# Two step boundaries between a norm and its transposes, and an order for the transposes, in the last attention of a sequence kernel

## The chip, the cores and the metric

The kernel runs on one core of a Trainium2 chip. A core has five engines that work side by side, each through its own instructions in order: TensorE (PE in the profile, with its weight loads shown apart as PEld), VectorE (DVE), ScalarE (ACT), GpSimd (POOL), and SyncE (SP), which here only issues DMAs. The metric is the device time of one execution in microseconds (us); lower is better.

## The reference, cut to what matters

The reference is a chain of eight residual layers on 8 sequences of 256 tokens with 128 channels, each followed by a layer norm without gain. The change touches the end of it: the mixture of experts that is the sixth layer (its norm), the attention that is the seventh, and the ternary linear layer that is the eighth. In the reference's words:

```
x = _layernorm(x + _L2_ffn_ref(x, ...))           # experts: shared + two routed per token
x = _layernorm(x + _L3_attn_ref(x, w_qkv, w_o, log_xi))
x = _layernorm(x + _L3_ffn_ref(x, weight, alpha, bias))
...
scores = einsum('bhqd,bhkd->bhqk', q, k) * dh ** (-0.5) + bias   # 16 heads of 8, causal, some heads with decay
attn = softmax(scores);  out = einsum('bhqk,bhkd->bhqd', attn, v);  return out @ w_o
```

So for every sequence there are three norms over channels in this last part: after the experts, after the attention, and after the linear layer.

## The kernel before, in words

The kernel runs six stages one after another. The change lies in the last two, `moe2` (the experts) and `typed` (the attention, with the linear layer behind it). A norm works with tokens on partitions, so that a token's mean and variance lie along one partition; the matmuls that follow need channels on partitions. Each norm is therefore followed by two 128x128 transposes on TensorE.

**The norm.** `token_norm` (L468) takes statistics for two blocks of 128 tokens on VectorE (L474, L475), a logarithm and an exponential on ScalarE for the reciprocal root (L477, L478), then gives control back once (`yield`), and then scales and shifts both blocks on VectorE (L481: two instructions in the profile's "L481 ... x2"). `channels` (L483) takes one PSUM bank (tag M, of which this stage has one), transposes the two blocks into it on TensorE (L487, tile `zt`) and copies the bank to SBUF (L488, on VectorE or ScalarE as its caller says).

**The turns of `typed`.** Each of the 8 sequences gives six units of attention: two for the first 128 queries (four pairs of heads each, 8 groups of 128 keys) and four for the second 128 queries (4 groups of 256 keys). The loop takes one turn `i` per unit and is software-pipelined. Turn `i` gives out, in this order:

1. the transposes of the weights of unit `i-3` (L507, tile `pt`, with copies `ptsb` at L509 on whichever of VectorE and ScalarE the scheduler picks);
2. the scores of unit `i` on TensorE (tile `sc`, two PSUM banks A in all);
3. the softmax of unit `i-1`: maximum on VectorE (L1766, `nm`), exponentials on ScalarE (L1771), reciprocal of the sums on VectorE (L1773, `rc`; this one is also remembered as `self.paced`), and the multiply by it on GpSimd (L1774, tile `e`);
4. two steps of side work;
5. the outputs of unit `i-3` on TensorE (tile `o`, 16 matmuls);
6. one more step of side work.

The side work comes from a queue of generators; a step runs the front one to its next `yield`. There are three kinds:

- `results(b)` finishes the experts of sequence b: four VectorE instructions that add two gathered, weighted rows to the shared part (L1638, "combine" below), the first norm, its transposes and the copy `x_moe`. The first instruction of each pair is held behind `self.paced`, the reciprocal given out last.
- `before(b)` makes that sequence's attention inputs: two projections (`proj`), the products for q and k, the masked keys `km` on GpSimd (L1726), and v.
- `after(b)`: the output projection (`wo`), residual and second norm (L1824, L474 to L481), its transposes and the copy `s_t`, a bias add on GpSimd (L1829), the linear layer (`lin`), residual (L1836), third norm, its transposes and the copy out.

I count turns within a sequence as turn 3 to turn 8: in turn 3 the outputs of a sequence's first unit come, in turn 8 those of its sixth. `results(b+2)` enters the queue in turn 3, `before(b+2)` and `after(b)` at the end of turn 8. The first sequence's `results` and first `before` run during the last parts of `moe2`, between the chunks of the shared expert (`shared`, L1550 and on: `pg`, `pu`, L1571 `sh`, `acc`), the second's at the start of `typed`.

**What sets the order.** The program order is a priority, not the final order. A compile-time scheduler walks a modelled time and gives each engine, whenever it is free, the ready instruction of highest priority; copies written as `nc.any` rank lower and go to either engine. The result is a fixed queue per engine, and on the chip an instruction that has to wait holds up all behind it on its engine. `issue_after(later, earlier)` adds an edge without a semaphore: it only forbids the scheduler to place `later` before `earlier`.

Of the kernel before, what the change touches and what calls it, by code (L numbers as in the profile page):

```python
# [21 lines left out]
P = 128  # L22
# [284 lines left out]
class _Kernel:  # L307
    def __init__(self, ctx, tc, ins, out):
# [67 lines left out]
        self.places = [self.dram.tile([2560, P], F32, name=f"places{i}") for i in range(2)]  # L376
        self.scatters = [], []


    def v(self, name, j=0, n=1):  # L380
        c = _V[name] + j
# [101 lines left out]
    def channels(self, z, dst, copy, tag="M"):  # L483

        ps = self.psum(tag, "zt")
        for t in range(2):
            self.nc.tensor.transpose(ps[:, t * P : (t + 1) * P], z[:, t, :], self.ident)  # L487
        copy(dst, ps[:, 0:S])  # L488

    def softmax(self, small, work, sc, groups, keys, tag):  # L490
# [1048 lines left out]
    def moe2(self):  # L1539
        nc, tc = self.nc, self.tc  # L1540
        E, CAP = 8, 320
        x = self.x
        y = self.xs.tile([P, T], F32, tag="x", name="x_moe2")
        ws = self.ws
        gu, down = self.wsh

        keep = self.pool("keep")
        self.typed_start()
        with (
            tc.tile_pool(reuse_waits="tile", name="m2", bufs=1) as one,  # L1550
            tc.tile_pool(reuse_waits="tile", name="m2w", bufs=2) as work,
        ):
            ss = []

            def shared(i):
                cs = bass.ts(i, 512)
                acc = self.psum("S", "acc")
                s = keep.tile([P, 4, P], F32, name=f"s{i}")
                nc.sync.dma_start(s, self.zrows[512 * i : 512 * (i + 1), :].rearrange("(t p) d -> p t d", p=P))
                ss.append(s)  # L1560
                for c in range(8):
                    pg, pu = self.psum("A", "pg"), self.psum("A", "pu")
                    self.mm(pg, gu[:, 0, c * P : (c + 1) * P], x[:, cs])
                    self.mm(pu, gu[:, 1, c * P : (c + 1) * P], x[:, cs])
                    h = work.tile([P, 512], F32, tag="sh", name="sh")
                    self.silu = nc.scalar.activation(h, pg, AF.Silu)
                    if self.norm:

                        self.issue_after([self.silu], self.norm)
                        self.norm = None  # L1570
                    self.paced = nc.vector.tensor_mul(h, h, pu)  # L1571
                    for t in range(4):
                        ts = slice(t * P, (t + 1) * P)
                        self.mm(acc[:, ts], h[:, ts], down[:, c * P : (c + 1) * P], c == 0 and t == 0, c == 7 and t == 3)
                    yield
                s = s.rearrange("p t d -> p (t d)")
                nc.vector.tensor_add(s, acc, s)


            self.norm = None  # L1580
            common = shared(0)
            for _ in range(2):
                next(common)
            for _ in self.rest:
                pass
            bt, group = self.rows_of(one, 1)
            for _ in common:
                pass
            ybuf = self.dram.tile([E * CAP, P], F32, name="ybuf2")
            groups = 0  # L1590
            for e in range(E):
                w = ws.pop(0) if ws else self.weights2(e)
                while 512 * groups < CAP * (e + 1):
                    group(groups)
                    groups += 1
                xe = bt[:, e * CAP : (e + 1) * CAP]
                h = work.tile([P, 4, CAP], F32, tag="h", name="h")
                for c in range(4):
                    pg, pu = self.psum("A", "pg"), self.psum("A", "pu")
                    self.mm(pg[:, :CAP], w[:, 0, c * P : (c + 1) * P], xe)  # L1600
                    self.mm(pu[:, :CAP], w[:, 1, c * P : (c + 1) * P], xe)
                    nc.scalar.activation(h[:, c, :], pg[:, :CAP], AF.Silu)
                    nc.vector.tensor_mul(h[:, c, :], h[:, c, :], pu[:, :CAP])
                ys = work.tile([P, 3, P], F32, tag="ys", name="ys")
                py = self.psum(name="py")
                for i, n in enumerate((P, P, CAP - 2 * P)):
                    for c in range(4):
                        self.mm(py[0:n, i * P : (i + 1) * P], h[:, c, i * P : i * P + n], w[:, 2, c * P : (c + 1) * P], c == 0, c == 3)
                nc.any.tensor_copy(ys[:, 0:2, :].rearrange("p a b -> p (a b)"), py[:, 0 : 2 * P])
                nc.any.tensor_copy(ys[0:64, 2, :], py[0:64, 2 * P : 3 * P])  # L1610
                r0 = e * CAP
                nc.sync.dma_start(ybuf[r0 : r0 + 2 * P, :].rearrange("(a p) d -> p a d", p=P), ys[:, 0:2, :])
                nc.sync.dma_start(ybuf[r0 + 2 * P : r0 + CAP, :], ys[0:64, 2, :])
            got = [[], []]

            def fetches():


                for t in range(NT):
                    for k in range(2):  # L1620
                        got[k].append(self.gather(keep, ybuf, self.get2[:, k], t, f"got{k}{t}"))
                        if t > 1:
                            self.wait_for(self.gathered, self.silu)
                            yield

            fetch = fetches()
            next(fetch)

            def results(b, work):

                z = self.rows(b)
                if b == 0:
                    self.exp_ln(self.silu)
                for j in range(2):
                    t = 2 * b + j
                    for k in range(2):

                        i = nc.vector.scalar_tensor_tensor(z[:, j, :], got[k][t], self.gate2[:, k, t : t + 1], z[:, j, :], ALU.mult, ALU.add)  # L1638
                        if k == 0:
                            self.issue_after([i], self.paced)  # L1640
                yield from self.token_norm(z, z, self.tys)
                yield
                self.channels(z, y[:, bass.ts(b, S)], nc.vector.tensor_copy)

            self.results = results
            self.rows = lambda b: ss[b // 2][:, b % 2 * 2 : b % 2 * 2 + 2, :]
            for _ in shared(1):
                next(fetch)
            self.x = y
            first = chain(results(0, self.ty), self.typed_before(0))  # L1650
            for i in (2, 3):
                for _ in shared(i):
                    next(first, None)
                    next(fetch, None)
            for _ in chain(first, fetch):
                pass
            self.exp_ln(self.silu)
# [83 lines left out]
    def typed_scores(self, unit, q, km, decay, last):  # L1741

        t, r0, r1 = unit
        keys, nr = P * (t + 1), r1 - r0
        sc = self.psum("A", "sc", 1024).rearrange("p (j r k) -> p j r k", j=2, r=nr)
        half = [slice(64 * j, 64 * j + 64) for j in range(2)]
        line = [self.mm(sc[:, j], q[h, t * P : (t + 1) * P], km[h, r0:r1, 0:keys], True, False) for j, h in enumerate(half)]
        for j, h in enumerate(half):  # L1750
            line.append(self.mm(sc[:, j, 1::2, :], self.onesb[h, :], decay[h, r0 // 2 : r1 // 2, 0:keys], False, False))
        for j in range(2):
            line.append(self.mm(sc[:, j, :, keys - P : keys], self.identb, self.m("causal").unsqueeze(1).to_broadcast([P, nr, P]), False, True))
        for i in line:
            if last is not None:
                self.issue_after([i], last)
            last = i
        return sc, last

    def typed_softmax(self, unit, sc, work, small):  # L1760
# [20 lines left out]
    def typed_outputs(self, unit, pts, vm, o, last):  # L1781
        t, r0, r1 = unit
        for i in range(4):
            r, kt = r0 + i // (t + 1), i % (t + 1)
            for j, pt in enumerate(pts):
# [6 lines left out]
                )  # L1792
                if last is not None:
                    self.issue_after([m], last)

    def typed_start(self):
        one, self.ty, self.tys = self.pool("ty1"), self.pool("ty", 2), self.pool("tys", 6)
# [11 lines left out]
    def typed(self):  # L1809
# [3 lines left out]
        def after(b, o):  # L1813
# [4 lines left out]
            ps = self.psum("M", "wo")[:, 0:S]  # L1818
            for t in range(2):
                ts = slice(t * P, (t + 1) * P)  # L1820
# [3 lines left out]
            nc.vector.tensor_add(flat(s), ps, flat(self.rows(b)))  # L1824
            yield from self.token_norm(s, s, small)
            yield
            st = work.tile([P, S], F32, tag="st", name="s_t")
            self.channels(s, st, nc.scalar.copy)
            nc.gpsimd.tensor_tensor(s, s, self.bias3.unsqueeze(1).to_broadcast([P, 2, P]), ALU.add)  # L1829
            yield  # L1830
            ps = self.psum("M", "lin")[:, 0:S]
            for t in range(2):
                ts = slice(t * P, (t + 1) * P)
                self.mm(ps[:, ts], st[:, ts], we, t == 0, t == 1)
            s2 = work.tile([P, 2, P], F32, tag="s2", name="s2")
            nc.vector.tensor_add(flat(s2), ps, flat(s))  # L1836
            yield from self.token_norm(s2, s2, small)
            yield
            s3 = work.tile([P, S], F32, tag="s3", name="s3")
            self.channels(s2, s3, nc.scalar.copy)  # L1840
# [75 lines left out]
```

## Time and profile before

| quantity | value |
|---|---|
| median of 3 runs | 1842.15 us (1837.2 to 1847.08) |
| the profiled execution's own time | 1842.98 us |
| span of the profiled execution | 1840.4 us |
| mean granted TensorE clock | 0.925 |
| PE busy over the span | 1529.9 us (83%) |
| DVE, ACT, POOL busy | 1111.1, 1002.1, 587.6 us |
| PE busy, 1680 to 1720 us | 36.84 of 40 us, granted clock 1.00 |
| PE busy, 1800 to 1841 us | 25.43 of 41 us, granted clock 0.86 |

The stage `typed` runs from about 1590 us to the end, at 29.1 us per sequence in the middle. A row of a timeline gives the start in us, the duration in us, the engine, the source line, the operation, output<-inputs, shapes and the count of merged instructions; in square brackets stands how long the engine was idle before, and what released it. A line such as L404 is a helper's, so one goes by the tile's name.

### The profile page before, as it was taken

Reading aid. Unit: us, or ns where it says so; the run is one execution under the profiler, and the core shown is the slowest. Engines: PE = TensorE matmul, PEld = TensorE weight load, DVE = VectorE, ACT = ScalarE, POOL = GpSimd, SP = SyncE. Lnnn points to the kernel's source line nnn. Section 1 sums busy time; section 2 is a strip of 40 time slices with the busy share of each in tenths; the row PEclk is TensorE's granted clock in tenths of the full one; section 3 lists DMA queues with packets and bytes.
Section 4 is the critical chain, followed back from the end, with each engine's and each line's share of the span. In section 5 each row is a group of like instructions: output and inputs, shape, how many; then the busy total and the mean of one; then the engine's idle time right before and its main releaser. Section 6 shows DMA issues by size and latency. Waiting matters only on the chain.

```text
span 1840.4 us, 28746 instructions
## 1 busy us (share of the span) xinstructions
PE 1529.9 (83%) x10858; PEld 941.3 (51%) x10858; DVE 1111.1 (60%) x2158; ACT 1002.1 (54%) x2690; POOL 587.6 (32%) x535
## 2 busy tenths in 40 slices
PE   3667887878788878778479999999996998899996
PEld 2244544544444444344266666666654665456564
DVE  5724458778787776967624556554545222577775
ACT  4556777667767795666134444444444222355553
POOL 1314434343434324110412122211213004456562
PEclk7798998989999989888779999999998999999998
DMA  4000002020202031246530000000101320000000
GB/s 178 1 1 1 1 23 59 13 70 24 70 24 70 24 92 36 58 153 207 133 105 7 4 13 10 9 4 8 40 4 36 79 67 26 18 4 4 7 7 6
DMA packets 63049, 77.97 MB, mean 42 GB/s; under 512 B 6108, under 2 KB 39924, under 8 KB 61888
## 3 DMA queue, kind: packets, MB, share of 16 engines
q1 hardware_dynamic: 57584, 70.03, 13.2%
q0 software_dynamic: 3216, 5.07, 1.0%
q8 instruction: 85, 1.39, 0.3%
q10 hardware_dynamic: 2112, 1.05, 0.2%
q14 instruction: 52, 0.43, 0.1%
HBM read 66.87 MB, written 10.76 MB: 42 GB/s over the span
## 4 chain that ended last, share of the span: by engine, by line
PE 50%; DVE 19%; ACT 12%; issue 8%; POOL 8%; DMA 2%; another core or an unknown queue 0%; SPq 0%; DVEq 0%; POOLq 0%; ACTq 0%
PE vps L404 7%; PE sc L404 6%; PE kps L404 5%; PE pt L507 4%; PE out L404 3%; DVE hs L832 3%; PE o L404 3%; PE pu L404 3%; ACT e L679 3%; PE pg L404 3%; DVE hs L833 2%; PE y L404 2%; DVE hs L830 2%; PE py L404 2%; PE hps L404 2%
## 5 line engine op out<-in xcount | busy, mean ns | idle before, releaser
L404 PE MATMUL y<-hs,ident 128*128 128x512 f32 x256 | 147.9, 707 | 40.3 <-DVE hs L833 40.0
L832 DVE TENSOR_TENSOR_SCAN hs<-da,hs 128x1024 f32<-128x1024 f32 x64 | 153.5, 2405 | 1.8 <-ACT da L828 1.6
L507 PE MATMUL pt<-ident,e 128*128 128x128 f32 x768 | 120.6, 287 | 28.0 <-POOL e L684 13.8
L684 POOL TENSOR_TENSOR e<-e,rc 128x1024 f32<-128x1024 f32 x32 | 67.7, 2116 | 234.0 <-DVE rc L683 233.8
L828 ACT ACTIVATE da<-d,na 128x255 f32<-128x255 f32 x256 | 111.8, 501 | 40.0 <-DVE hs L832 21.6
L1771 ACT ACTIVATE e<-sc,nm 128x128 f32<-128x128 f32 (+1 forms) x256 | 103.7, 432 | 44.8 <-DVE nm L1766 44.8
L679 ACT ACTIVATE e<-sc,nm,rn 128x128 f32<-128x128 f32 x256 | 113.4, 463 | 26.6 <-DVE nm L674 24.1
L507 PEld LDWEIGHTS pt<-ident,e 128*128 128x128 f32 x768 | 87.9, 144 | 66.0 <-issue 19.9
L631 POOL TENSOR_TENSOR t<-t,t 128x512 f32<-128x512 f32 x64 | 91.0, 1421 | 93.9 <-DVE t L618 78.3
L1774 POOL TENSOR_TENSOR e<-e,rc 128x1024 f32<-128x1024 f32 x48 | 92.0, 1918 | 90.0 <-DVE rc L1773 77.5
L830 DVE TENSOR_TENSOR hs<-u,bc 128x1024 f32<-128x1024 f32 x64 | 86.3, 1358 | 34.8 <-POOL u L817 29.4
L1322 ACT COPY kp<-kps 128x512 f32<-128x512 f32 x128 | 74.5, 585 | 54.5 <-PE kps L404 53.3
L1171 POOL DMA_INDIRECT got<-ybuf,get x48 | 45.8, 955 | 179.6 <-DMA ybuf<-ys 88.3
L404 PEld LDWEIGHTS y<-hs,ident 128*128 128x128 f32 x256 | 51.8, 217 | 98.5 <-DVE hs L833 54.9
L509 ACT COPY ptsb<-pt 128x512 f32<-128x512 f32 x91 | 53.2, 586 | 82.4 <-PE pt L507 73.2
L1347 POOL TENSOR_TENSOR e<-e,rc 128x512 f32<-128x512 f32 x32 | 33.5, 1048 | 198.7 <-DVE rc L1346 90.9
L509 DVE COPY ptsb<-pt 128x512 f32<-128x512 f32 x101 | 67.4, 678 | 33.5 <-PE pt L507 33.4
L404 PE MATMUL qk<-w_local,h 128*128 128x512 f32 x128 | 70.4, 638 | 14.1 <-DVE t L618 9.9
L833 DVE TENSOR_TENSOR hs<-hs,bc 128x1024 f32<-128x1024 f32 x64 | 80.2, 1259 | 0.2
L636 PE MATMUL qkt<-ident,t 128*128 128x128 f32 x256 | 44.0, 292 | 28.2 <-POOL t L633 20.4
L1571 DVE TENSOR_TENSOR sh<-sh,pu 128x512 f32<-128x512 f32 x32 | 22.0, 688 | 75.1 <-PE pu L404 56.6
L1358 ACT COPY vs<-vps 128x512 f32<-128x512 f32 x64 | 37.3, 583 | 54.4 <-PE vps L404 49.2
(384 smaller groups left out, 3868.4 us busy)
## 6 DMA issues: line engine op xcount, KB each, us to landing
bc<-xs SPq DMA_DIRECT2D x128, 256.0 KB
w_attn<-in_w_dram SPq DMA_DIRECT2D x4, 1024.0 KB
w_local<-in_w_dram SPq DMA_DIRECT2D x2, 1557.0 KB
places<-zeros SPq DMA_DIRECT2D x2, 1280.0 KB
w_moe<-in_e1gate_dram SPq DMA_DIRECT2D x8, 256.0 KB
w_moe<-in_e1up_dram SPq DMA_DIRECT2D x8, 256.0 KB
w_moe<-in_e1down_dram SPq DMA_DIRECT2D x8, 256.0 KB
w_moe<-in_e2rg_dram SPq DMA_DIRECT2D x8, 256.0 KB
```

The costliest lines, as they stand in the source:

```text
L404: return self.nc.tensor.matmul(out, lhsT, rhs, start=start, stop=stop)
L507: self.last = self.nc.tensor.transpose(pt[:, j * P : (j + 1) * P], src[:, j * P : (j + 1) * P], self.ident)
L509: self.nc.any.tensor_copy(sb.rearrange("p a b -> p (a b)"), pt)
L631: nc.gpsimd.tensor_add(t1, t1, t2)
L679: nc.scalar.activation(e[:, j, g, :], scs[:, j, g, :], AF.Exp, bias=nm[:, j, g : g + 1], scale=rq[:, j, g : g + 1], accum_out=sm[:, j, g : ...
L828: nc.scalar.activation(da[:, n, c, 1:S], d[:, c, 1:S], AF.Exp, scale=na[:, i : i + 1])
L830: nc.vector.tensor_tensor(hs, u.unsqueeze(1).to_broadcast(shp), bn, ALU.mult)
L832: nc.vector.tensor_tensor_scan(line(hs), line(da), line(hs), 0.0, ALU.mult, ALU.add)
L833: nc.vector.tensor_tensor(hs, hs, cn, ALU.mult)
L1322: self.copied = nc.scalar.copy(k[:, 2 * i : 2 * i + 2, :].rearrange("p a b -> p (a b)"), ps)
L1771: nc.scalar.activation(e[:, i, :], sc[:, i, :], AF.Exp, bias=nm[:, i : i + 1], accum_out=sm[:, i : i + 1])
L1774: nc.gpsimd.tensor_tensor(e, e, rc.unsqueeze(2).to_broadcast([P, n, keys]), ALU.mult)
```

## The change

It does two things. First, in the three places where a norm's scalings are followed by its transposes (`results`, and twice in `after`), a second `yield` stands between them, so that two boundaries between steps lie there and not one. Second, `channels` holds each transpose behind `self.fed`, the TensorE instruction that was given out last by the scores, the outputs or the shared expert's last matmuls, with an edge of order alone. `self.fed` is `None` until `shared` first runs, so an earlier caller of `channels` is untouched.

```diff
@@ __init__
         self.scatters = [], []
+        self.fed = None
@@ channels
         ps = self.psum(tag, "zt")
         for t in range(2):
-            self.nc.tensor.transpose(ps[:, t * P : (t + 1) * P], z[:, t, :], self.ident)
+            i = self.nc.tensor.transpose(ps[:, t * P : (t + 1) * P], z[:, t, :], self.ident)
+            if self.fed:
+                self.issue_after([i], self.fed)
         copy(dst, ps[:, 0:S])
@@ shared, in moe2
                         ts = slice(t * P, (t + 1) * P)
-                        self.mm(acc[:, ts], h[:, ts], down[:, c * P : (c + 1) * P], c == 0 and t == 0, c == 7 and t == 3)
+                        self.fed = self.mm(acc[:, ts], h[:, ts], down[:, c * P : (c + 1) * P], c == 0 and t == 0, c == 7 and t == 3)
@@ results, in moe2
                 yield from self.token_norm(z, z, self.tys)
                 yield
+                yield
                 self.channels(z, y[:, bass.ts(b, S)], nc.vector.tensor_copy)
@@ typed_scores
             last = i
+        self.fed = last
         return sc, last
@@ typed_outputs
                     self.issue_after([m], last)
+        self.fed = m
@@ after, in typed
             yield from self.token_norm(s, s, small)
             yield
+            yield
             st = work.tile([P, S], F32, tag="st", name="s_t")
...
             yield from self.token_norm(s2, s2, small)
             yield
+            yield
             s3 = work.tile([P, S], F32, tag="s3", name="s3")
```

## The prediction

> **What bounds the kernel now.** I read the page's engine row, then the busy time by stretches of the last attention, then what TensorE waited for there, then the timeline of one sequence.
>
> ```profile
> PE 1529.9 (83%) x10858; PEld 941.3 (51%) x10858; DVE 1111.1 (60%) x2158; ACT 1002.1 (54%) x2690; POOL 587.6 (32%) x535
> ```
>
> ```profile
> 1680.00:1720.00 40.00, 36.84 (x298) 23.84 (x300) 30.32 (x68) 25.71 (x120) 23.09 (x15) 1.00 0.01 4
> 1800.00:1841.00 41.00, 25.43 (x206) 16.89 (x202) 19.92 (x46) 13.82 (x53) 10.92 (x7) 0.86 0.02 7
> ```
>
> The columns of the stretches are width, then busy time of PE, PEld, DVE, ACT and POOL, then granted clock, DMA share and GB/s. In the steady part TensorE is busy 36.84 of 40 us; no other engine passes 31. So TensorE's idle gaps are all that there is to win there. The waits of TensorE, 1611 to 1800 us, have one row for our transposes (total, times, longest):
>
> ```profile
> PE zt L487 <- DVE s L481: 11.2, 18, 1.4
> ```
>
> The timeline shows where they fall. One sequence of 29.1 us, TensorE first, in turns 6 to 8:
>
> ```profile
> 1646.45 0.49 PE L487 MATMUL zt<-ident,s 128*128 128x128 f32 x2 [0.42 <-DVE s L481]
> 1646.87 1.09 PE L404 MATMUL o<-ptsb,vm 128*64 128x128 f32 x16
> ...
> 1650.09 0.61 PE L404 MATMUL sc<-msk,identb 128*128 128x512 bf16 x2
> 1652.10 0.59 PE L487 MATMUL zt<-ident,s 128*128 128x128 f32 x2 [1.40 <-DVE s L481]
> 1652.61 1.09 PE L404 MATMUL o<-ptsb,vm 128*64 128x128 f32 x16
> ```
>
> The first wait is the third norm's (of `after`), the second the first norm's (of `results`). The VectorE and GpSimd rows say why the second is long:
>
> ```profile
> 1645.96 0.60 DVE L481 TENSOR_SCALAR s<-s,mv,rs 128x128 f32<-128x128 f32 x2
> 1646.47 0.17 DVE L1773 RECIPROCAL rc<-sm 128x4 f32<-128x4 f32 x1
> 1646.56 2.75 DVE L1638 SCALAR_TENSOR_TENSOR s<-got,gate,s 128x128 f32<-128x128 f32 x4
> ...
> 1650.90 0.66 DVE L509 COPY ptsb<-pt 128x512 f32<-128x512 f32 x1
> 1651.70 0.60 DVE L481 TENSOR_SCALAR s<-s,mv,rs 128x128 f32<-128x128 f32 x2
> ```
>
> ```profile
> 1646.79 2.11 POOL L1774 TENSOR_TENSOR e<-e,rc 128x1024 f32<-128x1024 f32 x1 [3.06 <-DVE rc L1773]
> ```
>
> The combine takes 2.75 us here while GpSimd multiplies; at 1588.16, with no such multiply running, the same four took 1.13. It loses 1.62 us, and it does so because it stands right behind a reciprocal, which releases a multiply 0.3 us later. The scalings L481 show the same: 0.60 alone, 1.86 at 1610.51 and 1.82 at 1804.23, where a reciprocal had just gone.
>
> The gaps, listed: 1.40 five times (1652 to 1768), 0.42 six times (1646 to 1792), 0.15 six times (second norm), 0.83 once at 1612.18: 7.0 + 2.5 + 0.9 + 0.8 = 11.2, the row above. Outside it: 1.70 and 1.90 at 1805.94 and 1812.94 for the last sequence but one; 2.20 and 2.27 for the last, which has nothing left to put in between; 0.50 and 0.52 around the transposes at 1544.24 in the experts' stage. All that can move adds to 7.0 + 2.5 + 0.9 + 0.8 + 3.6 + 1.0 = 15.8 us, 0.86% of the time.
>
> **The change part by part.** No arithmetic instruction is added or removed; the edges are order on one engine and need no semaphore, cost 0.
>
> *Does the side queue hold?* A generator takes its yields plus one step. `results` goes from 3 to 4, `after` (its first step is taken at once) from 7 to 9, `before` stays 5: 15 become 18, and a sequence has 6 turns of 3 steps, 18. It just fits, so nothing piles up; but the queue no longer runs empty, and this moves the start of `results` too. Before, the combine was given out at the end of turn 6, behind the reciprocal of turn 6; now `after` is not done until turn 7, so the combine comes in turn 7, behind turn 7's reciprocal. Its transposes come in turn 8, not 7. The boundary bought is partly spent at the start of the chain. The other moves: the linear layer goes from the middle of turn 5 to its end, behind the outputs; the third norm's scaling from the end of turn 5 to turn 6, its transposes to the end of turn 6, behind the outputs; the store (SP's queue) to turn 7, where the transposes' result is ready and nothing waits for it. GpSimd's queue keeps its order except at the start. `before` stays in its place, at the end of turn 8.
>
> *Third norm, six times.* Its scaling ends at 1646.5 while the 16 outputs (1.02) now run first. The outputs need their copies `ptsb`, the last of which ends at 1646.03, so they run 1646.1 to 1647.1, and the transposes find their input there: 0.35 of 0.42 gained, -2.1. Ends: -2.5; or, if the reciprocal goes ahead of the scaling, it grows by 1.26 (1.86 less 0.60), reaches 1647.9, and the gap is 0.8: +2.3.
>
> *The linear layer behind the outputs.* Its result is awaited by the residual add L1836, which waits longer for the bias add on GpSimd (1643.00 + 0.73). `lin` would end at about 1643.3: cost 0. Were that add earlier, up to 0.8 (the ten outputs moved ahead) would fall on the third norm, and the 1.02 of outputs ahead of its transposes would take it up.
>
> *First norm, five times.* Scores in turn 6 end at 1645.95. Turn 7's maximum, no longer behind the combine, takes 1646.6 to 1647.8, its 8 exponentials about 3.0 (0.34 to 0.41 apiece): the reciprocal goes at about 1651.0 and the combine right behind it, with the multiply on its heels: 2.75, to 1653.9. Statistics and ScalarE's two take 1.2, the scaling 0.60: transposes at 1655.75 at the earliest. TensorE, 0.35 early, has turn 8's scores done at 1653.95 and the outputs at 1654.97. So at least 0.8 us of gap is left: -0.6 each, -3.0. From above: the two `ptsb` copies of turn 8 (1.3) and a maximum (1.2) want VectorE in the same stretch behind the blocked combine; with the copies alone the scaling ends at 1657.1 and the gap is 3.2, +1.8 each, +9.0. Between these ends I take 1.6, the part of the combine that only the multiply explains: the schedule is made without it, I infer, for its order would otherwise not leave TensorE idle there; whatever place it picks, this lag lands on TensorE. That is +0.2 each, +1.0.
>
> The Trainium skill, "SBUF — State Buffer", section "Who interferes with whom", speaks against the change here: VectorE (with two SBUF inputs) and GpSimd share a port pair as an exclusive lock, and the loser blocks for the whole instruction. The combine would then cost 1.13 + 1.89 = 3.02 where the row says 2.75, and this sum would be 0.27 x 5 = 1.4 us worse; the row decides.
>
> *Second norm, six times:* same order (scores, transposes, outputs): 0.
>
> *Last sequence but one.* The first gap, 1.70, gets the other 14 outputs (about 0.95) ahead of it: -0.95. The second transposes come a whole turn later: -1.90. Together -2.85; some comes back, as TensorE then waits for the last softmaxes (0.35, 0.23 and 0.29 from 1819 on): I take -2.0, ends 0 and -3.6.
>
> *Start.* At 1612.18 ten more outputs (0.80) go ahead: -0.8, ends 0 and -0.83. The second sequence's first transposes move behind the scores of the next unit and push `km` (3.75 on GpSimd) later; TensorE waits 2.80 at 1606.61 for a multiply behind it. Either that multiply slips ahead (-2.8) or another falls behind (+1.9, one multiply). Between the two: 0.
>
> *Experts' stage.* One chunk later the scaling is long done: -0.5; ends 0 and -1.0, both gaps.
>
> Sum: -2.1 + 1.0 - 2.0 - 0.8 - 0.5 = -4.4 us. The profiled execution took 1842.98 (its span is 1840.4), which gives 1838.6; that execution is 0.83 above the median of the runs, which gives 1837.8. I say 1838.
>
> **The rivals.**
>
> *The gaps close (gain over 0.5%).* For it: two boundaries give 1.02 to 4.7 us more work ahead of the transposes. Against: the combine's later reciprocal. With the lower ends, -2.1 - 3.0 - 2.85 - 0.8 - 1.0 - 2.8 = -12.6: 1830; if the 7.0 vanish whole, -16.6: 1826. It holds from the point where the first norm's scaling ends before 1655.0 on the old scale.
>
> *The gap widens in turn 8 (slower).* The copies `ptsb` queue behind the blocked combine, TensorE stands 3.2 us: +9.0. After the 2.80 gap at 1606.61 the next scores took 2.60 from start to outputs (1607.63 to 1610.23) against 1.50 at 1614.51, and the stretch 1600 to 1640 has a granted clock of 0.96 against 1.00: +1.1 each, +5.5. With the other terms (-5.4): +9.1, 1852 by the profile's time, 1851 by the median. For it: VectorE's full stretch; against: gaps of 1.70 and 1.90 slowed nothing. It is slower than before when the gap passes 1.40 by 1.1 (5.4 over five).
>
> The Trainium skill, "TensorE: Matmul & The Clock Gate", section "Why this matters for your kernels", puts the drop of the clock at idle gaps above about 3 us; here 2.80 already slowed it. By the page the 5.5 stays for a gap of 3.2 and falls away for one of 2.8.
>
> *The order comes out as before,* if the scheduler's times leave the transposes where they were: 1842.
>
> **How the numbers follow.** Chances: forecast 0.40, gaps close 0.28, gap widens 0.22, no change 0.10. The forecast's own range is 1834 to 1842: the term of the first norm between -3.0 and +5.0 (a gap of 2.4), the rest as summed. The whole range is 1828 to 1854: below to the middle of the first rival, above to the second with the start's +1.9. Half a per cent, 9.2 us, is about what a measurement of this kernel can tell from no change. Faster than that: the first rival and a little of the forecast, 0.30; slower: most of the second, 0.22; within: 0.48.
>
> **What would show it.** Right: the transposes of the third norm stand behind 16 outputs with no gap; the combine stands behind a reciprocal of 128x8, not 128x4, at 2.75 again; the gap of 1.40 turns up in turn 8, before `zt` or `o`, at about 1.6. Wrong: a period clearly under 28.6 or over 30 us; `ptsb` copies on ScalarE all through turn 8; a granted clock under 1.00 in the steady part; scalings of 1.8 in it.

## The result, and the profile after

The changed kernel takes **1871.11 us** (median of 4 runs, 1868.33 to 1873.65), the kernel before, run beside it, 1844.62 us (1837.2 to 1847.74): a ratio of **1.0143**, 95% interval 1.0123 to 1.0162. It is slower by some 26.5 us. The forecast was 1838 and the range ended at 1854, so the prediction was wrong in sign and in size. The second rival named the place of the loss, but priced it at 1851.

The profiled execution of the changed kernel took 1872.6 us, its span is 1870.7. Engine row of its page:

```profile
PE 1546.2 (83%) x10858; PEld 956.9 (51%) x10858; DVE 1111.0 (59%) x2151; ACT 1005.2 (54%) x2697; POOL 584.0 (31%) x535
```

TensorE issues the same 10858 matmuls, but they take 16.3 us longer (1546.2 against 1529.9), and idle time has been added too. Busy time by stretches of the last attention (columns as in the prediction: width, PE, PEld, DVE, ACT, POOL, granted clock, DMA share, GB/s):

```profile
1680.00:1720.00 40.00, 35.11 (x268) 23.11 (x266) 26.84 (x63) 21.79 (x95) 21.75 (x15) 0.91 0.01 4
...
1760.00:1800.00 40.00, 33.87 (x256) 21.47 (x252) 26.95 (x61) 20.72 (x91) 19.10 (x12) 0.91 0.01 5
```

Two things at once: TensorE is busy for 35 of 40 us where it was 37, and its clock is 0.91 where it was 1.00. It also gets less done while busy: 268 matmuls against 298. The 0.91 is a mean: the granted clock is 0.51 from 1664.5 to 1671.3 us, from the last microsecond of a long gap on, and 1.00 from 1671.4 to 1698.7. TensorE's waits, in a window that lies where the one shown of before lay (everything is 7 us later here):

```profile
PE zt L489 <- DVE s L483: 26.9, 16, 3.6
```

It was 11.2 us, longest 1.4; it is now 26.9, longest 3.6. (L489 is the old L487, L483 the old L481.) The timeline of TensorE, turns 6 to 8 of one sequence:

```profile
1653.19 1.09 PE L406 MATMUL o<-ptsb,vm 128*64 128x128 f32 x16
1655.26 0.49 PE L489 MATMUL zt<-ident,s 128*128 128x128 f32 x2 [0.97 <-DVE s L483]
...
1661.48 0.39 PE L406 MATMUL sc<-msk,identb 128*128 128x256 bf16 x2
1665.49 0.47 PE L489 MATMUL zt<-ident,s 128*128 128x128 f32 x1 [3.61 <-DVE s L483]
...
1666.92 1.97 PE L406 MATMUL o<-ptsb,vm 128*64 128x128 f32 x14
1668.82 1.33 PE L511 MATMUL pt<-ident,e 128*128 128x128 f32 x5
1669.94 1.80 PE L406 MATMUL proj<-x_moe,w 128*128 128x256 f32 x4
```

The third norm's transposes do stand behind 16 outputs now, and still TensorE waits 0.97 us (0.42 before). The first norm's stand behind turn 8's scores, and TensorE waits 3.61 us (1.40 before). After that gap four projections take 1.80 us; they take 1.13 where no long gap came before. VectorE in the same stretch:

```profile
1652.91 0.15 DVE L1779 RECIPROCAL rc<-sm 128x4 f32<-128x4 f32 x1
1653.64 1.73 DVE L483 TENSOR_SCALAR s<-s,mv,rs 128x128 f32<-128x128 f32 x2 [0.51 <-ACT rs L480]
1655.29 1.21 DVE L1772 TENSOR_REDUCE nm<-sc 128x8 f32<-128x1024 f32 x1
...
1659.53 0.20 DVE L1779 RECIPROCAL rc<-sm 128x8 f32<-128x8 f32 x1 [1.83 <-ACT e L1777]
1659.65 2.73 DVE L1642 SCALAR_TENSOR_TENSOR s<-got,gate,s 128x128 f32<-128x128 f32 x4
...
1662.78 1.19 DVE L1772 TENSOR_REDUCE nm<-sc 128x8 f32<-128x1024 f32 x1
1663.89 0.17 DVE L477 BATCH_NORM_AGGREGATE mv<-st 128x2 f32<-128x6 f32 x1
1665.09 0.60 DVE L483 TENSOR_SCALAR s<-s,mv,rs 128x128 f32<-128x128 f32 x2 [1.03 <-ACT rs L480]
```

and GpSimd's two multiplies of that stretch:

```profile
1653.14 1.89 POOL L1780 TENSOR_TENSOR e<-e,rc 128x1024 f32<-128x1024 f32 x1 [1.67 <-DVE mv L477]
...
1659.81 1.90 POOL L1780 TENSOR_TENSOR e<-e,rc 128x1024 f32<-128x1024 f32 x1 [4.78 <-DVE rc L1779]
```

Read from the top: the reciprocal now goes *ahead* of the third norm's scaling. It releases a multiply at 1653.14 (the profile names `mv`, the aggregate that ended 0.07 us after the reciprocal), and the scaling beside it takes 1.73 us instead of 0.60. That delays the transposes (the 0.97) and the maximum `nm` of turn 7 behind it. So turn 7's reciprocal comes late, at 1659.53. The combine, right behind it, meets the next multiply (2.73). A maximum of the next unit is wedged into the norm's statistics (1662.78), and ScalarE's two steps of the norm each come behind an exponential (VectorE idle 1.03). Each of these stands between the combine and the transposes for which TensorE waits.

**Where the 30.3 us between the two spans lie.**

| stretch, by its first and last instruction | before | after | difference |
|---|---|---|---|
| start to the first `acc` after the long wait in the experts' stage | 1530.72 | 1536.17 | +5.45 |
| from there to the first `sc` of `typed` | 59.62 | 62.01 | +2.4 |
| to the first `proj` of the third sequence | 37.74 | 37.64 | -0.1 |
| five sequences, `proj` to `proj` (29.1 and 34.2 each) | 145.5 | 170.85 | **+25.3** |
| from there to the end | 66.8 | 64.0 | -2.8 |

The first row is not the change's: the instructions there stand in the same order in both kernels, and the granted clock differs from the start of the run on. Without it the sum is 24.9, beside the 26.5 of the medians. The five sequences are the case. Their +5.1 each are +2.2 at the first norm's gap, +0.55 at the third's, and some +2.3 of matmuls that take longer at the lower clock (the remainder).

### The profile page after: what moved, and what is told of

Its sections match the earlier page's. It is cut to its first block, busy times and chain, and to the rows that moved or that the text cites. A ratio compares the mean times of both kernels' runs of the same rounds, so it can differ in the third digit from the quotient of the medians.

```text
span 1870.7 us, 28734 instructions
## 1 busy us (share of the span) xinstructions
PE 1546.2 (83%) x10858; PEld 956.9 (51%) x10858; DVE 1111.0 (59%) x2151; ACT 1005.2 (54%) x2697; POOL 584.0 (31%) x535
## 3 DMA queue, kind: packets, MB, share of 16 engines
q10 hardware_dynamic: 2112, 1.05, 0.2%
## 4 chain that ended last, share of the span: by engine, by line
PE 48%; DVE 20%; ACT 14%; issue 8%; POOL 8%; DMA 2%; another core or an unknown queue 0%; SPq 0%; DVEq 0%; POOLq 0%; ACTq 0%
PE vps L406 7%; PE kps L406 5%; PE sc L406 5%; PE out L406 3%; PE pt L511 3%; DVE hs L836 3%; PE o L406 3%; PE pu L406 3%; ACT e L683 3%; PE pg L406 3%; ACT e L1777 2%; DVE hs L837 2%; DVE hs L834 2%; PE y L406 2%; PE py L406 2%
## 5 line engine op out<-in xcount | busy, mean ns | idle before, releaser
L511 PE MATMUL pt<-ident,e 128*128 128x128 f32 x768 | 125.5, 294 | 22.9 <-POOL e L688 12.0
L683 ACT ACTIVATE e<-sc,nm,rn 128x128 f32<-128x128 f32 x256 | 113.4, 463 | 24.9 <-DVE nm L678 22.3
L511 PEld LDWEIGHTS pt<-ident,e 128*128 128x128 f32 x768 | 91.8, 149 | 62.5 <-issue 20.4
L1351 POOL TENSOR_TENSOR e<-e,rc 128x512 f32<-128x512 f32 x32 | 33.5, 1048 | 197.1 <-DVE rc L1350 89.4
L513 DVE COPY ptsb<-pt 128x512 f32<-128x512 f32 x94 | 62.9, 681 | 43.8 <-PE pt L511 43.6
L640 PE MATMUL qkt<-ident,t 128*128 128x128 f32 x256 | 44.8, 296 | 26.5 <-POOL t L637 19.1
L1362 ACT COPY vs<-vps 128x512 f32<-128x512 f32 x64 | 37.3, 583 | 54.4 <-PE vps L406 49.2
```

The source lines that it names most:

```text
L511: self.last = self.nc.tensor.transpose(pt[:, j * P : (j + 1) * P], src[:, j * P : (j + 1) * P], self.ident)
L513: self.nc.any.tensor_copy(sb.rearrange("p a b -> p (a b)"), pt)
L683: nc.scalar.activation(e[:, j, g, :], scs[:, j, g, :], AF.Exp, bias=nm[:, j, g : g + 1], scale=rq[:, j, g : g + 1], accum_out=sm[:, j, g : ...
```

## Experiments

Three questions were open. Which part of the change does it: the moved steps, the boundaries, or the edges on PE? Is it the multiply on GpSimd that makes combine and scaling long? And is the slow clock an effect of the gaps? In the tables "steady period" is the mean over the five sequences from the third's first projection, and "to the end" goes from there to the last instruction, so that a different clock earlier in the run is left out.

| kernel | ratio to before, 95% interval | steady period | to the end |
|---|---|---|---|
| before (profile shown) | 1 | 29.1 | 212.3 |
| the change | 1.0143 (1.0123 to 1.0162) | 34.2 | 234.9 |
| boundary in `results` alone | 1.0003 (0.9976 to 1.0031) | 28.8 | 211.0 |
| boundaries in `after` alone | 1.0118 (1.0078 to 1.0157) | 33.8 | 233.2 |
| one empty step | 1.0113 (1.0077 to 1.0149) | 32.0 | 226.9 |
| the change without edges | 1.0128 (1.0096 to 1.0160) | 34.0 | 234.0 |
| the change, small multiply | 0.9927 (0.9899 to 0.9956) | 29.1 | 205.8 |
| before, small multiply | 0.9887 (0.9853 to 0.9921) | 26.7 | 196.9 |
| the change, gap filled | 1.0080 (1.0052 to 1.0108) | 32.2 | 226.6 |
| the change, `results` started in turn 6 | 0.9953 (0.9935 to 0.9971) | 28.3 | 204.6 |
| before, multiply held | 0.9960 (0.9938 to 0.9981) | 27.5 | 205.5 |
| the change, started in turn 6 and held | 0.9912 (0.9885 to 0.9940) | 26.6 | 196.4 |

### One part of the change at a time

The boundary in `results` alone. This diff, and each one below where nothing else is said, is against the changed kernel; the edge on PE stays in:

```diff
@@ after, in typed: the two added boundaries taken out
             yield from self.token_norm(s, s, small)
             yield
-            yield
...
             yield from self.token_norm(s2, s2, small)
             yield
-            yield
```

> Only the boundary in results and the edge; after has one boundary in each norm as before. Slot theory (the two steps added to after push the combine from turn 6 to turn 7, and that is the loss): the combine stays at the end of turn 6 behind a reciprocal of 128x4, the period stays at or under 29.1 us, the time is -6 to +2 us against the kernel before. Rival (the transposes' new place, behind work given out last, makes the gaps): the gap before zt in turn 7 or 8 is 3 us or more and the time is +15 us or more.

And the boundaries in `after` alone:

```diff
@@ results, in moe2
                 yield from self.token_norm(z, z, self.tys)
                 yield
-                yield
                 self.channels(z, y[:, bass.ts(b, S)], nc.vector.tensor_copy)
```

> Only the two boundaries in after and the edge; results has one boundary as before. Slot theory: the combine comes in turn 7 all the same, gaps of about 3.6 us before zt, period 33 to 34 us, +18 to +28 us. Rival (the boundary in results is the fault): -3 to +5 us.

Measured: 1848.86 us for the first and 1866.32 for the second, against 1845.40 for the kernel before on the same chip. In the first the combine keeps its place in turn 6 behind the reciprocal of 128x4 (2.75 us), the third norm's gap is 0.42 as before, and the gap of the first norm moves from the transposes to the outputs ahead of them, shorter:

```profile
1665.76 1.09 PE L406 MATMUL o<-ptsb,vm 128*64 128x128 f32 x14 [0.55 <-DVE ptsb L513]
1666.78 0.44 PE L489 MATMUL zt<-ident,s 128*128 128x128 f32 x2
```

In the second, where `results` is as before, its combine has moved nevertheless, and the gaps are 0.97 and 3.61 us, those of the whole change:

```profile
1681.77 0.49 PE L489 MATMUL zt<-ident,s 128*128 128x128 f32 x2 [0.97 <-DVE s L483]
...
1691.99 0.47 PE L489 MATMUL zt<-ident,s 128*128 128x128 f32 x1 [3.61 <-DVE s L483]
```

So most of the loss comes with the boundaries in `after`, and the larger part of it falls on another generator's norm, one that was not edited.

### One empty step in the queue

The kernel before with a bare step ahead of the store in `after`: no boundary between a norm and its transposes, no edge. The queue then has 16 steps for its 18 places in place of 15.

```diff
@@ after, in typed
+            yield
             nc.sync.dma_start(self.out[:, cs], s3)
```

> The kernel before with one empty step in after, just ahead of its store: no norm has a second boundary and no transpose has an edge; only what comes behind after in the queue moves one step. Slot theory: this alone moves the combine to turn 7 behind a reciprocal of 128x8; period 31 to 34 us, +10 to +25 us. Rivals (boundaries or edge at fault): the time of the kernel before within 4 us.

Measured: 1861.71 us, ratio 1.0113. VectorE and then TensorE, turns 7 and 8:

```profile
1653.42 0.20 DVE L1773 RECIPROCAL rc<-sm 128x8 f32<-128x8 f32 x1 [0.90 <-ACT e L1771]
1653.55 2.73 DVE L1638 SCALAR_TENSOR_TENSOR s<-got,gate,s 128x128 f32<-128x128 f32 x4
...
1656.68 1.18 DVE L1766 TENSOR_REDUCE nm<-sc 128x8 f32<-128x1024 f32 x1
...
1658.98 0.60 DVE L481 TENSOR_SCALAR s<-s,mv,rs 128x128 f32<-128x128 f32 x2 [1.03 <-ACT rs L478]
```

```profile
1649.09 0.49 PE L487 MATMUL zt<-ident,s 128*128 128x128 f32 x2 [0.42 <-DVE s L481]
...
1659.38 0.33 PE L487 MATMUL zt<-ident,s 128*128 128x128 f32 x1 [2.82 <-DVE s L481]
```

A step that does nothing costs most of what the change costs. It pushes the start of `results` out of turn 6: the combine stands behind turn 7's reciprocal of 128x8, and the first norm's gap is 2.82 us. The third norm, whose steps have not moved, keeps 0.42 and a scaling of 0.60. Against turn 8's scores the combine starts 1.1 us earlier here than in the change (1.77 us ahead of them, not 0.66), which is about what the blocked scaling of the third norm adds there (1.73 for 0.60). In the gap 0.79 of it shows (3.61 less 2.82), since the last two score matmuls, 0.3 us, stand behind the first transpose here and ahead of it in the change. Here the clock comes and goes: it was 1.00, 0.91, 0.88 and 0.95 in four stretches of 40 us from 1640 on, and the sequences took 30.3 to 33.0 us.

### The change without the edges

```diff
@@ channels
         for t in range(2):
-            i = self.nc.tensor.transpose(ps[:, t * P : (t + 1) * P], z[:, t, :], self.ident)
-            if self.fed:
-                self.issue_after([i], self.fed)
+            self.nc.tensor.transpose(ps[:, t * P : (t + 1) * P], z[:, t, :], self.ident)
```

> The three boundaries without the edge of order. Slot theory: as the change, +20 to +30 us, since the transposes are late by their data. Rival (the edge holds them behind outputs and so makes the gaps): under +8 us.

Measured: 1868.24 us, ratio 1.0128; the gaps are 0.97 and 3.61 again. In the last attention the edges do nothing that the boundaries would not do alone. In the experts' stage they do something. TensorE there, first in the change, then without the edges:

```profile
1548.25 1.02 PE L406 MATMUL pu<-x_chunked,w_shared 128*128 128x512 f32 x2
1551.29 1.39 PE L406 MATMUL pg<-x_chunked,w_shared 128*128 128x512 f32 x2 [2.02 <-ACT sh L1570]
1552.48 1.92 PE L406 MATMUL acc<-w_shared,sh 128*128 128x128 f32 x8
```

```profile
1549.14 1.02 PE L406 MATMUL pu<-x_chunked,w_shared 128*128 128x512 f32 x2
1550.66 0.58 PE L489 MATMUL zt<-ident,s 128*128 128x128 f32 x2 [0.50 <-DVE s L483]
1551.77 1.13 PE L406 MATMUL proj<-x_moe,w 128*128 128x256 f32 x4 [0.52 <-DVE x_moe L490]
```

Without the edge the transposes and the projections stand in the wait for `sh`, at two gaps of 0.5 us. With it they are kept behind the next chunk's last `acc`, and TensorE idles 2.02 us in one piece, after which `acc` takes 1.92 in place of 1.16. Every kernel here that has the edge has this gap, and none without it. From the long wait to the first scores of `typed` the change needs 62.01 us, before needed 59.62. Of this 2.4 us only some 0.6 is the idle time: where the clock stood at 1.00 throughout, the same stretch took 57.88 us with the edge (boundaries in `after` alone) and 57.24 without (this run). The rest goes with the clock, which fell behind the 2.02 us in five of the seven kernels that have this gap; in the other two (boundaries in `after` alone, and the gap filled, below) the same `acc` took 1.05.

### The multiply made small

GpSimd multiplies 8 columns of each group of 128 or 256, so this leaves out most of the softmax's scaling; everything else is issued as before. Once in the changed kernel, once in the kernel before, with the same edit:

```diff
@@ typed_softmax
-        nc.gpsimd.tensor_tensor(e, e, rc.unsqueeze(2).to_broadcast([P, n, keys]), ALU.mult)
+        nc.gpsimd.tensor_tensor(e[:, :, 0:8], e[:, :, 0:8], rc.unsqueeze(2).to_broadcast([P, n, 8]), ALU.mult)
```

> The changed kernel with GpSimd's multiply by the reciprocals cut to 8 columns of each group (the rest of the softmax stays unscaled, so the output is another). Port theory (the long gaps are VectorE's combine and scaling standing still while GpSimd multiplies): the combine takes 1.1 us and not 2.7, the scaling 0.6 and not 1.7, the gap before the third norm's transposes falls from 0.97 to under 0.1 and the one of turn 8 from 3.6 to under 1.2, the granted clock is 1.00 again, and the time is -8 to +4 us against the kernel before. Rival (the order of the queues on VectorE and ScalarE alone): gap of turn 8 over 2.5 us, time +12 us or more.

> The kernel before with the same cut of GpSimd's multiply. Port theory: the combine takes 1.1 us, the gap of 1.40 us before the first norm's transposes is gone, 29.1 us per sequence become 27.7 or less, -7 to -16 us. Rival: within 3 us of the kernel before.

Measured: 1826.39 and 1817.28 us against 1839.89 for the kernel before on the same chip: ratios 0.9927 and 0.9887. The changed kernel, VectorE and then TensorE:

```profile
1667.24 0.20 DVE L1779 RECIPROCAL rc<-sm 128x8 f32<-128x8 f32 x1 [1.48 <-ACT e L1777]
1667.36 1.13 DVE L1642 SCALAR_TENSOR_TENSOR s<-got,gate,s 128x128 f32<-128x128 f32 x4
...
1671.19 0.60 DVE L483 TENSOR_SCALAR s<-s,mv,rs 128x128 f32<-128x128 f32 x2 [1.03 <-ACT rs L480]
```

```profile
1663.56 0.44 PE L489 MATMUL zt<-ident,s 128*128 128x128 f32 x2
1671.60 0.33 PE L489 MATMUL zt<-ident,s 128*128 128x128 f32 x1 [1.47 <-DVE s L483]
```

The combine stands behind the reciprocal as in the change and takes 1.13 us, not 2.73; the scalings take 0.60; the third norm's gap is gone. So it is the multiply beside them that makes them long, not their place on VectorE. Both times fell further than expected (-13.5 and -22.6 us), in part because the shorter multiply also shortens the first two sequences (37.6 us to 33.5 in the changed kernel, from the first scores to the third sequence). What is left of the first norm's gap, 1.47 (under 1.2 was expected), is the order alone: the maximum between the statistics and the 1.03 us for ScalarE are still there. The clock did not quite come back to 1.00 either: it was 0.96 in two of the four stretches of 40 us from 1640 on. The kernel before, without the long multiply, loses both its gaps: its combine takes 1.11 and a sequence 26.7 us in place of 29.1. The changed one stays 8.9 us behind it from the third sequence to the end (205.8 against 196.9), which is what the changed order costs with the blocking nearly gone, the dips of the clock included.

The first rule that the prediction drew on, in the Trainium skill, "SBUF — State Buffer", section "Who interferes with whom", has the loser blocked for the whole instruction. The runs agree: the combine is 1.60 us longer beside a multiply of 1.90 (2.73 against 1.13 beside a short one). Taken singly, nearly all of this falls on the second of its four instructions: in the changed kernel it began at 1659.87, 0.06 us after the multiply, took 1.99 us where the others took 0.30 to 0.34, and ended 0.15 us after the multiply did.

### The gap filled

The changed kernel with 11 matmuls of the identity ahead of the first norm's transposes in the last five sequences, into the same bank, overwritten later (the profile shows each as two, 22):

```diff
@@ channels, with fill=11 from results where b > 2
+        for _ in range(fill):
+            i = self.mm(ps[:, S : S + P], self.ident, self.ident)
+            self.issue_after([i], self.fed)
         for t in range(2):
```

> The changed kernel with 11 matmuls of the identity by itself (about 0.27 us each by the rows of the linear layer, 3.0 us) put ahead of the first norm's transposes for the last five sequences; their result is overwritten. Clock theory (TensorE's gap of 3.6 us slows the matmuls after it, 2.3 us per sequence): the gap is filled to under 1 us, proj after it takes 1.1 and not 1.8 us, the period falls from 34.2 to about 32 us, the time is 8 to 13 us under the changed kernel's, at +12 to +19 us, although 55 matmuls are added. Rival (the slow rows have another cause): as the changed kernel or slower, +26 us or more.

Measured: 1854.58 us, ratio 1.0080: 55 matmuls more, and faster than the change by 0.6 of a per cent. TensorE:

```profile
1678.76 2.62 PE L406 MATMUL zt<-ident 128*128 128x128 f32 x22
1682.53 0.59 PE L492 MATMUL zt<-ident,s 128*128 128x128 f32 x2 [1.15 <-DVE s L483]
...
1684.76 1.13 PE L406 MATMUL proj<-x_moe,w 128*128 128x256 f32 x4 [0.63 <-DVE x_moe L495]
```

The transposes come no earlier than their input, but TensorE is never idle for more than 1.2 us here (under 1 was expected), the projections take 1.13 and not 1.80, and the granted clock in the four stretches from 1640 is 0.96 to 1.00 in place of 0.91. Most of the slow clock is thus an effect of the gap. Four of the five sequences took 31.9 us, 2.3 less than the change's 34.2: that is the +2.3 per sequence of the table above. One took 33.5: even behind a gap of 1.15 us the clock fell, twice in five times and for 3.4 us, half as long as behind the change's 3.61. Over the whole the filling brings back 0.0063 of 1845 by the ratios, 11.6 us (their intervals leave 5 to 18), and 8.3 us by the column "to the end".

### `results` started by hand in turn 6

If the place in the queue is the cause, the change should do well with that place restored. The changed kernel, all boundaries and edges kept, but `results(b+2)` begun at the end of turn 6, past the queue:

```diff
@@ the loop of typed, in turn 3
-                    if b + 2 < B:
-                        side.append(self.results(b + 2, work))
@@ the same loop, after the last step of side work
+            if i >= 3 and u[:2] == (1, 2) and b + 2 < B:
+                side.append(self.results(b + 2, work))
+                next(side[-1])
```

> The changed kernel, all three boundaries and the edge, but each results is started by hand at the end of turn 6, as late as in the kernel before, and waits in the queue only for its other steps. Slot theory: the combine stands behind a reciprocal of 128x4 again and the transposes of turn 8 have no gap; what is left is the third norm's gap of up to 1 us; period 28 to 30 us, -6 to +6 us against the kernel before. Rival (the boundaries themselves cost): +12 us or more.

Measured: 1829.65 us, ratio 0.9953, faster than both. TensorE:

```profile
1646.84 0.49 PE L489 MATMUL zt<-ident,s 128*128 128x128 f32 x2 [1.64 <-DVE s L483]
...
1653.55 0.38 PE L489 MATMUL zt<-ident,s 128*128 128x128 f32 x2
```

The first norm's transposes in turn 8 run with no gap, and the time is better than the range that was expected (-10.2 us). But the third norm's wait 1.64 us, where up to 1 was expected: on VectorE three of the four combines now go ahead of its scaling, and beside a multiply they take 2.48 us.

### The multiply held

The last two runs take the shared stretch away without leaving work out: GpSimd's multiply of that turn waits until the combine's last instruction is done. Once on the kernel before, once on the kernel of the last section; this diff is against the former.

```diff
@@ results, in moe2, behind the combine's last instruction i
+                if b > 2:
+                    self.wait_for(self.scaled, i)
@@ typed_softmax
-        nc.gpsimd.tensor_tensor(e, e, rc.unsqueeze(2).to_broadcast([P, n, keys]), ALU.mult)
+        self.scaled = nc.gpsimd.tensor_tensor(e, e, rc.unsqueeze(2).to_broadcast([P, n, keys]), ALU.mult)
```

> The kernel before, with one wait more: from the third sequence on, GpSimd's softmax multiply of turn 6 starts only when VectorE's combine L1638 (its last instruction) is done. No arithmetic is changed. If the shared stretch is what makes the combine long in the kernel before (2.75 us beside the multiply, 1.13 alone), the combine takes about 1.1 us, the scaling comes 1.6 us earlier, the gap of 1.40 us ahead of the first norm's transposes in turn 7 goes, a sequence takes at most 27.8 us instead of 29.1, and the whole 7 to 12 us less than before. If the hold costs as much as it gives (the multiply ends 1.1 us later, and pt L507 behind it waits), the gap moves to pt with about 1 us, and the time stays within 3 us of before.

> The changed kernel with results started by hand in turn 6, as in e8_started_in_turn6, and with the multiply of that turn held until the combine is done. If the 1.64 us gap that was left ahead of the third norm's transposes comes from the combine that the multiply blocks (2.48 us), it falls under 0.4, a sequence takes 26.6 to 27.0 us, and the whole is 14 to 20 us faster than before. If it comes from the order on VectorE alone (combine ahead of the scaling), the gap stays over 1 us and the time is that of e8_started_in_turn6, 6 to 10 us faster than before.

Measured: 1839.81 and 1831.75 us against 1846.72 (-6.9, just under the 7 to 12 that were expected, and -15.0): ratios 0.9960 and 0.9912. The kernel before with the hold, first VectorE and GpSimd, then TensorE:

```profile
1682.77 1.11 DVE L1638 SCALAR_TENSOR_TENSOR s<-got,gate,s 128x128 f32<-128x128 f32 x4
...
1684.03 1.89 POOL L1776 TENSOR_TENSOR e<-e,rc 128x1024 f32<-128x1024 f32 x1 [4.09 <-DVE s L1638]
```

```profile
1682.66 0.49 PE L487 MATMUL zt<-ident,s 128*128 128x128 f32 x2 [0.42 <-DVE s L481]
...
1686.75 0.51 PE L487 MATMUL zt<-ident,s 128*128 128x128 f32 x2
```

The combine takes 1.11, the gap of 1.40 is gone, and the multiply, which goes about 1 us later than without the hold (1684.03, where the reciprocal ahead of it began at 1682.68 and 0.32 us lay between the two before), holds nothing up on TensorE. With the start in turn 6 as well, the third norm's gap goes too:

```profile
1680.02 1.09 PE L406 MATMUL o<-ptsb,vm 128*64 128x128 f32 x16
1681.13 0.49 PE L489 MATMUL zt<-ident,s 128*128 128x128 f32 x2
...
1687.84 0.38 PE L489 MATMUL zt<-ident,s 128*128 128x128 f32 x2
```

```profile
1680.00:1720.00 40.00, 39.82 (x329) 26.03 (x330) 31.86 (x79) 26.18 (x123) 24.58 (x16) 1.00 0.02 8
```

TensorE is busy for 39.82 of 40 us, a sequence takes 26.6 us, and the kernel is 15 us (0.9%) faster than before. From the third sequence to the end this is the time of the kernel before with the small multiply (196.4 against 196.9 us), with the whole multiply in it. The order on VectorE is that of the last section, three combines ahead of the scaling; they take 0.85 us here, not 2.48. So the 1.64 us of the last section was the blocked combine, not VectorE's order.

## Why the prediction was wrong, step by step

**The side queue: right as a mechanism.** Fifteen steps become 18, the combine moves to turn 7 behind the reciprocal of 128x8, and takes 2.73 (2.75 foreseen). The empty step shows that this alone costs 1.1%. The prediction saw the move and then priced it too low.

**Third norm, -2.1 taken, ends -2.5 and +2.3: wrong.** The step that failed is "its scaling ends at 1646.5": that the scaling would stay ahead of the reciprocal. It had been given out ahead of the softmax, and one boundary later it is given out behind it, so the reciprocal and its multiply go first: 1.73 us for the scaling, a gap of 0.97 in place of none. The upper end was the right case (a gap of 0.8 foreseen there). Five sequences cost +2.8. What the step did not see at all is that the same blocked scaling stands ahead of turn 7's maximum, so that the first norm's combine comes 0.8 us later than foreseen.

**First norm, +0.2 each, ends -3.0 and +9.0: mis-sized, and the main step that failed.** The measured gap is 3.61, that is +2.2 each, +11.1. On the new scale (7.7 us later) the chain of the lower end had turn 8's outputs done at 1662.7 and the transposes at 1663.5, a gap of 0.78. The runs show what is missing:

- The combine ends 0.78 later, behind the delayed maximum (with the third norm undisturbed, in the run with the empty step, the gap is 0.79 shorter).
- From the combine's end to the scaling it is 2.71 us, not 1.25: a maximum of 1.1 between the statistics and the aggregate, and 0.35 more for ScalarE's two steps, each behind an exponential.
- The first transpose needs only the first of the two scalings, which gives back 0.2.
- The 16 outputs that were to run ahead of the transposes come behind them, which leaves TensorE 0.79 more to wait. By the prediction's own count of steps the transposes are given out in the second step of turn 8, ahead of its outputs; the lower end put the outputs first.

0.78 + 0.78 + 1.46 - 0.20 + 0.79 = 3.61. The second item could have been read before the run. In the kernel before, the combine ends at 1649.31 and the scaling starts at 1651.70, 2.39 us later and not 1.25, and the maximum stands between the two aggregates there too:

```profile
1649.71 1.19 DVE L1766 TENSOR_REDUCE nm<-sc 128x8 f32<-128x1024 f32 x1
1650.82 0.17 DVE L475 BATCH_NORM_AGGREGATE mv<-st 128x2 f32<-128x6 f32 x1
```

The upper end, a gap of 3.2, was built on the two copies `ptsb` alone, without the maximum. In the run both copies go to ScalarE (1659.98 and 1660.47) and the maximum is what stands there, so that it came near is in part luck. The value taken between the ends, 1.6, came from the thought that the schedule hides all but the multiply's part. That thought has no row behind it. The run with the small multiply refutes it: with the blocking nearly gone, 1.47 us of gap remains.

**The clock, +1.1 each in the rival, left out of the forecast: mis-sized.** It came, at about +2.3 each, and the run with the filled gap shows that most of it follows from the gap. The rival's 1.1 was read from one gap of 2.80 in a stretch at 0.96; the steady part fell to 0.91.

**Experts' stage, -0.5, and edges at cost 0: wrong.** It cost +2.4. An edge of order took no time of its own here, but it forbade the work that filled a wait: the 2.02 us gap, 0.6 us more idle time, and the slower clock behind it. The prediction looked at what the transposes wait for and not at what waits behind them to fill TensorE.

**Last sequence but one, -2.0 taken, -2.85 worked out: the size came, partly by luck.** The end came 2.8 us sooner, but TensorE's idle time from there on fell by 1.2 us only (10.6 to 9.3): in place of 0.42, 1.70 and 1.90 stand 0.97, 0.38, 1.04 and 0.62. The rest is shorter busy time (51.3 to 49.2), in part the clock's, which is at half for the last 10.7 us before and for the last 8.1 now. **Start, -0.8 taken, -0.1 measured: near, by luck.** The gap of 0.83 that was to go grew to 3.17, and that of 2.80 went. **Linear layer and second norm, 0: right;** in the period nothing of theirs shows (the second norm's gap is 0.15 as before).

All the signs that the prediction named for its own failure came: a period over 30 us (34.2), the copies of turn 8 on ScalarE, a clock under 1.00 (0.91), scalings of 1.7. With the sizes measured (first norm +11.1, clock +11.5, third norm +2.8, experts' stage +2.4, start -0.1, last sequence but one -2.8) the second rival's sum is +24.9 us; with the numbers on record it was +9.1. The clock's 11.5 is what remains of the five sequences' 25.3, so this sum comes out by its making; its check is the run with the filled gap.

What stays open: why the scheduler places the last maximum between the statistics and the aggregate was not tried, and so the 1.47 us that this order costs without blocking has no run that removes it by itself. Nor does a run show what makes the clock fall behind one gap and not behind another of the same length.

## What to carry to other kernels

In a queue of side work a boundary is not free even if it is empty: count which generator is pushed out of its place, and read what stands ahead of it there. Before moving a VectorE instruction, look which GpSimd instruction is released just ahead of it; a wait that keeps the long GpSimd instruction back for one microsecond was worth 7 us here, and 15 with the order mended. And price an idle gap on TensorE twice, once by its length and once by the matmuls behind it: here 3.61 us of gap cost some 2.3 us more behind it.

## What the hardware showed that I had not expected

The matmuls behind gaps of 3.61 us (`proj` 1.80 for 1.13) ran slower each time, behind 2.82 us in four sequences of five, and behind 2.0 us (`acc` 1.92 for 1.16) in five kernels of seven; behind 1.40 and 1.64 us they did not. The length of the gap does not decide alone: in the changed kernel with the small multiply, whose gaps are 1.47 us, the clock fell behind two of five, and a gap of 3.18 us at 1617.97 in the change without edges left it at 1.00. Five gaps of 3.61 us held the mean granted clock at 0.91 from 1640 us to the end of the five sequences, and matmuls of no use in the gap brought back 2.3 us in each of four sequences. The Trainium skill, "TensorE: Matmul & The Clock Gate", section "Why this matters for your kernels", puts the limit at about 3 us; these rows put the first slow matmuls lower.

And the shared stretch was not a loss of the change alone: in the kernel before it cost 1.6 us of each period (29.1 against 27.5 with the hold).
